# The decayed factors of the queries: from a transfer of their own to two ScalarE exponentials a chunk

## The chip, the core and the metric

The kernel runs on one core of a Trainium2 chip. A core has five engines that each run their own instructions in order and wait for one another by semaphores: PE (TensorE, matmuls; its weight loads are listed as PEld), DVE (VectorE), ACT (ScalarE), POOL (GpSimd) and SP (SyncE, which here issues most transfers). Transfers are carried out by 16 DMA engines. The metric is the device time of one execution in microseconds (us), the median of the runs.

## The reference

One transformer block over `x` of shape 8 x 2048 x 256. The part that the change touches is the attention, a linear attention with a decay for each head (16 heads of 64 columns) and each token:

```python
h = layernorm(x) * (1 + ca) + sa
q = elu(h @ Wq) + 1 ; k = elu(h @ Wk) + 1 ; v = h @ Wv
a = sigmoid(h @ Wa + ba + 2)          # one decay for each head and token
for t in range(2048):                  # for each batch and head
    S = a[t] * S + outer(k[t], v[t]) ; z = a[t] * z + k[t]
    out[t] = (q[t] @ S) / (q[t] @ z + 1e-6)
x = x + ga * (out @ Wo)
```

After it come a second layer norm and a mixture of 8 experts (256 x 256 each), of which every token uses two, and a second gated addition.

## The kernel before, in words

The 2048 tokens of a batch are cut into groups of 256 tokens (`GT`), and a group into two chunks of 128 tokens (`C`). There are 64 groups. The recurrence is done by chunks: inside a chunk the scores of keys and queries are multiplied by the decay between the two tokens and by the values; what comes from earlier chunks is the state `S` multiplied by the queries, each query having been multiplied by the decay since the chunk's start.

Both decays come from one row for each head, `le`, the running sum of the negative logarithms of the decays in the chunk. `decays` (L343 to L381) makes it on a tile of 64 rows (two chunks of 32 rows), and before the change also its exponential `exp(-le)` as a second plane of the same tile (L371). Both planes go to a DRAM tensor `led` (L374). `chunk_decays` (L400 to L418) is a generator that a chunk advances in steps:

1. it issues the transfer of `le` for all 16 heads to all 128 partitions, into `dec` (128 x 2048, 1 MB, L405);
2. it issues two transfers of `exp(-le)`, each of eight heads to one half of the partitions, into `el` (128 x 1024, twice 256 KB, through `spread_pairs`, L395): partitions 0 to 63 hold the first head of each pair, 64 to 127 the second;
3. POOL replaces the entries of `dec` above the diagonal in place by a large number (`affine_select`, L409);
4. in four steps of four heads, ACT makes `dec = exp(-dec + lt)` in place (L415), the decay between two tokens.

`el` is then read by POOL: its last column becomes the chunk's `whole` decay (L1056), and `el` is multiplied by the queries in place (L1048). PE reads it in `from_state` (L548). `dec` is multiplied by the scores on DVE (L501) and read by PE in `outputs` (L565).

The order of the instructions on every engine is the order in which the program is written (a manual schedule); nothing is moved by a scheduler. One pass of the main loop works on several groups at once: `here` (the scores, values and state of its chunks c0 and c1), `ahead` (the next group: its keys and queries), `coming` (the one after: its decays) and `prev` (the last one: its expert routing). Between them stand up to five places in a pass where an expert tile is loaded, turned and applied (`expert_tiles`), and `fetch_outputs`, which gathers expert results with indirect transfers from POOL. Two places of a pass matter here, both of them a single `advance` of `chunk_decays`:

- **`advance(own)`**, after c0's values and the layer norm rows of `prev`, and ahead of c0's `from_state` and `outputs`. It does step 3 for c1. ACT's neighbours there are `lnn_f` (L288) before, and after it eight of the exponentials of step 4 and then `lowk`, the first of four evictions of the key projection (L336, L337). ACT's next work is `hT_f` (L308).
- **`advance(dk)`**, after the last key projection of `ahead` and ahead of its query projection. It does step 3 for the next c0. ACT's neighbours there are the copy `z` (L1148) before, and `lowq`, the first of four evictions of the query projection, after.

The projections `pk` and `pq`, the value projection `pv`, the expert tiles' `pxt` and `py`, and the output projection `pw` take turns in four PSUM buffers of one pool (`mm`). A matmul into a buffer waits until the tile that was in it has been read. For a key or query projection that is done by DVE, after ACT's relu and exponential (`kT` and `qT`, L338).

## Time and profile before

| | |
|---|---|
| Median of 3 runs | 3899.13 us (3888.24 to 3919.3) |
| Profiled execution | 3885.85 us, span of the trace 3884.1 us, mean granted PE clock 0.969 |
| Busy: PE / DVE / ACT / POOL | 91% / 68% / 54% / 48% |
| Moved by DMA | 712.09 MB, mean 183 GB/s |
| `dec<-led` | 128 transfers of 1024 KB |
| `el<-led` | 256 transfers of 256 KB |
| Exponentials into `dec` (ACT, L415) | 2048, 389 ns each |
| `affine_select` of `dec` (POOL, L409) | 128, 2007 ns each |

Busy time is the time in which an engine had an instruction of its own in progress. Instructions on one engine overlap a little, so that eight exponentials of 389 ns take 2.44 us and not 3.11. A line of the timeline gives start, duration, engine, source line, operation, out<-in with the shapes, and how many alike were merged; in brackets stands the idle time of the engine before it and what ended that idle time. "issue" is idle time for which the profile shows no wait.

### The profile page before, as it was taken

The numbers are of one execution on the slowest core, as the hardware profiler recorded it, in microseconds if no ns is written. First come the engines' busy times: TensorE is split into PE (matmuls) and PEld (weight loads), VectorE is DVE, ScalarE is ACT, GpSimd is POOL, SyncE is SP. The second block draws the span as 40 slices with busy tenths as digits, with TensorE's granted clock in tenths as the row PEclk, the third lists the DMA queues.
The fourth block names the chain that finished last, engine by engine and source line by source line (L and its number), as shares of the span: only waits on it lengthen the run. The fifth ranks groups of instructions, "written<-read, shape, count | busy, mean of one in ns | idle before, by whom it ended". The sixth has DMA issues, their size and how long they took to land.

```text
span 3884.1 us, 82134 instructions
## 1 busy us (share of the span) xinstructions
PE 3546.7 (91%) x28998; PEld 2742.2 (71%) x28998; DVE 2640.0 (68%) x6396; ACT 2083.2 (54%) x5423; POOL 1846.2 (48%) x1986
## 2 busy tenths in 40 slices
PE   5999999999999999999999998999999999788786
PEld 3777777777777777777777776777777777666665
DVE  3777777777667667667766767767767767556555
ACT  3555555655555645655555655555655555444442
POOL 1444443443555454454545546445455444444554
PEclk9999999999999999999999999999999999989898
DMA  6444457666676666676576676576576576666766
GB/s 188 130 122 133 133 148 194 196 176 170 196 217 175 186 179 193 182 216 185 161 222 188 181 192 188 172 209 190 171 209 195 164 205 180 200 190 197 212 199 189
DMA packets 347404, 712.09 MB, mean 183 GB/s; under 512 B 43736, under 2 KB 212968, under 8 KB 322416
## 3 DMA queue, kind: packets, MB, share of 16 engines
q1 hardware_dynamic: 313488, 625.52, 57.5%
q0 software_dynamic: 27264, 74.49, 5.6%
q10 hardware_dynamic: 6240, 6.84, 0.6%
q8 instruction: 229, 3.75, 0.4%
q14 instruction: 183, 1.50, 0.1%
HBM read 577.29 MB, written 132.53 MB: 183 GB/s over the span
## 4 chain that ended last, share of the span: by engine, by line
PE 64%; DVE 15%; ACT 7%; issue 6%; DMA 3%; POOL 2%; SPq 0%; another core or an unknown queue 0%; DVEq 0%; ACTq 0%; POOLq 0%
PE pv L528 10%; PE pw L615 9%; PE pq L326 7%; PE pk L326 7%; PE po L565 6%; PE py L886 5%; PE sc L492 4%; PE ps L599 3%; PE po L548 3%; DVE at L433 3%; PE pd L449 2%; PE pk L511 2%; DMA xg<-xrows 2%; POOL at L1154 2%; ACT dec L415 2%
## 5 line engine op out<-in xcount | busy, mean ns | idle before, releaser
L415 ACT ACTIVATE dec<-dec,lt 128x128 f32<-128x128 f32 x2048 | 628.5, 389 | 14.2 <-POOL dec L409 14.2
L1154 POOL TENSOR_TENSOR at<-at,qT 128x512 f32<-128x512 f32 x256 | 326.1, 1285 | 579.2 <-DVE rmark L715 401.6
L326 PE MATMUL pk<-hT_a,wk_sb 128*128 128x256 f32 x2048 | 512.8, 395 | 5.0 <-issue 4.7
L326 PE MATMUL pq<-hT_a,wq_sb 128*128 128x256 f32 x2048 | 482.2, 389 | 13.2 <-DVE kT L338 12.5
L615 PE MATMUL pw<-wo_sb,oT 128*128 128x256 f32 x2048 | 478.0, 388 | 4.7 <-DVE oT L577 4.7
L528 PE MATMUL pv<-wv_sb,hT_a 128*128 128x512 f32 x1024 | 472.3, 604 | 2.5 <-DVE yg L890 2.3
L326 PEld LDWEIGHTS pq<-hT_a,wq_sb 128*128 128x128 f32 x2048 | 392.0, 194 | 75.4 <-DVE kT L338 19.4
L875 ACT ACTIVATE xgT<-pxt,modT,modT 128x128 f32<-128x128 f32 x622 | 245.0, 447 | 358.4 <-PE pxt L870 336.6
L615 PEld LDWEIGHTS pw<-wo_sb,oT 128*128 128x128 f32 x2048 | 393.5, 195 | 59.2 <-DVE oT L577 5.5
L326 PEld LDWEIGHTS pk<-hT_a,wk_sb 128*128 128x128 f32 x2048 | 381.1, 196 | 70.3 <-issue 13.3
L886 PE MATMUL py<-we,xgT 128*128 128x256 f32 x1244 | 348.4, 405 | 62.1 <-ACT xgT L875 28.3
L409 POOL TENSOR_SCALAR_AFFINE_SELECT dec<-dec 128x2048 f32<-128x2048 f32 x128 | 256.9, 2007 | 266.4 <-DMA dec<-led 201.8
L577 DVE TENSOR_TENSOR oT<-po,rb 128x512 f32<-128x512 f32 x256 | 173.1, 690 | 296.2 <-PE po L565 119.2
L433 DVE TENSOR_TENSOR_SCAN at<-at,z,kT 128x256 f32<-128x256 f32 x448 | 353.7, 830 | 2.0
L501 DVE TENSOR_TENSOR dec<-sc,dec 128x512 f32<-128x512 f32 x512 | 327.3, 682 | 36.8 <-PE sc L492 35.2
L528 PEld LDWEIGHTS pv<-wv_sb,hT_a 128*128 128x128 f32 x1024 | 189.8, 192 | 216.7 <-issue 174.2
L620 POOL TENSOR_TENSOR xt<-xt,dx 128x256 f32<-128x256 f32 x128 | 94.3, 737 | 480.2 <-DVE dx L619 479.9
L565 PE MATMUL po<-dec,v 128*64 128x128 f32 x4096 | 272.3, 278 | 36.1 <-issue 26.0
L886 PEld LDWEIGHTS py<-we,xgT 128*128 128x128 f32 x1244 | 227.5, 200 | 103.6 <-ACT xgT L875 35.7
L492 PE MATMUL sc<-qT,kT 64*128 64x128 f32 x4096 | 298.1, 286 | 0.1
L492 PEld LDWEIGHTS sc<-qT,kT 64*128 64x128 f32 x4096 | 250.1, 188 | 63.0 <-issue 62.8
L336 ACT ACTIVATE lowk<-pk 128x512 f32<-128x512 f32 x256 | 152.3, 595 | 257.0 <-PE pk L326 218.8
(199 smaller groups left out, 6208.2 us busy)
## 6 DMA issues: line engine op xcount, KB each, us to landing
dec<-led SPq DMA_DIRECT2D x128, 1024.0 KB
we<-ew_d SPq DMA_DIRECT2D x311, 384.0 KB
at<-ad SPq DMA_DIRECT2D x128, 512.0 KB
el<-led SPq DMA_DIRECT2D x256, 256.0 KB
rb<-rdd SPq DMA_DIRECT2D x128, 512.0 KB
xg<-xrows SPq DMA_DIRECT2D x311, 128.0 KB
yrows<-yg SPq DMA_DIRECT2D x311, 128.0 KB
xt<-in_L_attn_x_dram SPq DMA_DIRECT2D x64, 256.0 KB
```

The lines of the kernel that those rows point to most:

```text
L326: nc.tensor.matmul(pp[:, j * GT : (j + 1) * GT], w[:, k, (jj + j) * P : (jj + j + 1) * P], hT[:, k, :], start=(k == 0), stop=(k == KD - 1),)
L409: nc.gpsimd.affine_select(out=dec, in_=dec, compare_op=ALU.is_ge, fill=1e30, base=0, pattern=[[0, H], [1, C]], channel_multiplier=-1,)
L415: nc.scalar.activation(dec[:, h, :], dec[:, h, :], AF.Exp, scale=-1.0, bias=x.lt[:, 0, ch, h : h + 1])
L433: nc.vector.tensor_tensor_scan(zz[:, j, :], at[:, j, :], kT[:, j, :], 0.0 if z is None else z[:, j : j + 1], ALU.mult, ALU.add,)
L492: nc.tensor.matmul(sc[q][:, i, :], self.kT[rows, half * 4 + i, self.tok], self.qT[rows, half * 4 + i, self.tok], start=True, stop=True,)
L501: nc.vector.tensor_mul(w4, sc[q], w4)
L528: nc.tensor.matmul(pv, self.hT[:, k, self.tok], wv_sb[:, k, i * 512 : (i + 1) * 512], start=(k == 0), stop=(k == KD - 1),)
L565: nc.tensor.matmul(po[half * DH : (half + 1) * DH, i, :], self.v[:, h * DH : (h + 1) * DH], self.dec[:, q * NP + j, :], start=(self.S is N ...
L615: nc.tensor.matmul(pw[:, :D], self.oT[:, j, :], wo_sb[:, j, :], start=(j == 0), stop=(j == NP - 1))
L875: nc.scalar.activation(self.xT[:, k, :], pt[:, k * P : (k + 1) * P], AF.Identity, bias=modT[3][:, k, b : b + 1], scale=modT[4][:, k, b : b ...
L886: nc.tensor.matmul(py[:, :D], self.xT[:, k, :], self.w[:, k, :], start=(k == 0), stop=(k == KD - 1))
L1154: nc.gpsimd.tensor_mul(zz[:, part, :], zz[:, part, :], ahead.qT[:, part, :])
```

## The change

The exponentials `exp(-le)` are no longer made on the 64-row tile and no longer sent through DRAM. In their place ACT makes them from `dec`, which holds `le` on all partitions before POOL masks it: two instructions a chunk, each on 64 partitions and 8 heads x 128 tokens. `le` and `led` lose their second plane, the two transfers into `el` and the generator's step for them are gone, and the step of `affine_select` now begins with the two exponentials.

```diff
-        le = wk2.tile([R2, 2, C], F32, tag="le", name=f"le_{tag}", bufs=2)
-        nc.vector.tensor_tensor_scan(le[:, 0, :], ones[:R2, :C], e, 0.0, ALU.mult, ALU.add)
+        le = wk2.tile([R2, C], F32, tag="le", name=f"le_{tag}", bufs=2)
+        nc.vector.tensor_tensor_scan(le, ones[:R2, :C], e, 0.0, ALU.mult, ALU.add)
...
         yield
-        nc.scalar.activation(le[:, 1, :], le[:, 0, :], AF.Exp, scale=-1.0)
-
-        led = dram.tile([2, R2, C], F32, tag="led", name=f"led_{tag}", bufs=4)
-        nc.sync.dma_start(out=led.rearrange("n r t -> r n t"), in_=le)
+
+        led = dram.tile([R2, C], F32, tag="led", name=f"led_{tag}", bufs=4)
+        nc.sync.dma_start(out=led, in_=le)
...
-        nc.sync.dma_start(out=dec, in_=led[0, ch * 32 : ch * 32 + H, :].partition_broadcast(P))
+        nc.sync.dma_start(out=dec, in_=led[ch * 32 : ch * 32 + H, :].partition_broadcast(P))
         yield dec, el
-        spread_pairs(el, led[1, ch * 32 : ch * 32 + H, :])
-        yield
+
+        for q in range(2):
+            part = slice(q * DH, (q + 1) * DH)
+            nc.scalar.activation(
+                el[part], dec[part, q * NP : (q + 1) * NP, :], AF.Exp, scale=-1.0
+            )
         nc.gpsimd.affine_select(
             out=dec, in_=dec, compare_op=ALU.is_ge, fill=1e30, base=0,
             pattern=[[0, H], [1, C]], channel_multiplier=-1,
...
                 dk = chunk_decays(ahead.led, ahead, 0)
                 ahead.dec_el[0] = next(dk)
-                next(dk)
...
                 ahead.rb = next(dn)
-                next(ahead.dk)
```

More of the change, by code (lines that the diff above doesn't have):

```diff
@@ L362, in decays @@
         nc.vector.tensor_sub(e, e, y)
-        le = wk2.tile([R2, 2, C], F32, tag="le", name=f"le_{tag}", bufs=2)
-        nc.vector.tensor_tensor_scan(le[:, 0, :], ones[:R2, :C], e, 0.0, ALU.mult, ALU.add)
+        le = wk2.tile([R2, C], F32, tag="le", name=f"le_{tag}", bufs=2)
+        nc.vector.tensor_tensor_scan(le, ones[:R2, :C], e, 0.0, ALU.mult, ALU.add)
         left = wk2.tile([R2, C], F32, tag="left", name=f"left_{tag}", bufs=1)
         nc.vector.tensor_tensor(
-            left, le[:, 0, :], le[:, 0, C - 1 : C].to_broadcast([R2, C]), ALU.subtract
+            left, le, le[:, C - 1 : C].to_broadcast([R2, C]), ALU.subtract
         )
         yield
-        nc.scalar.activation(le[:, 1, :], le[:, 0, :], AF.Exp, scale=-1.0)
-        led = dram.tile([2, R2, C], F32, tag="led", name=f"led_{tag}", bufs=4)
-        nc.sync.dma_start(out=led.rearrange("n r t -> r n t"), in_=le)
+        led = dram.tile([R2, C], F32, tag="led", name=f"led_{tag}", bufs=4)
+        nc.sync.dma_start(out=led, in_=le)
         nc.scalar.activation(left, left, AF.Exp)
@@ L385, in by_token @@
         pc = small_tile(f"pc_{tag}")
-        nc.tensor.transpose(pc[:, :R2], le[:, 0, :], ident[:R2, :R2])
+        nc.tensor.transpose(pc[:, :R2], le, ident[:R2, :R2])
         nc.tensor.transpose(pc[:, R2 : 2 * R2], left, ident[:R2, :R2])
```

## The prediction

> **What bounds the kernel.** I read the page first: its busy row, and the chain of work that ended last by engine.

> ```profile
> PE 3546.7 (91%) x28998; PEld 2742.2 (71%) x28998; DVE 2640.0 (68%) x6396; ACT 2083.2 (54%) x5423; POOL 1846.2 (48%) x1986
> ...
> PE 64%; DVE 15%; ACT 7%; issue 6%; DMA 3%; POOL 2%; SPq 0%; another core or an unknown queue 0%; DVEq 0%; ACTq 0%; POOLq 0%
> ```

> PE is the bound, so nothing counts until it reaches PE. ACT's 46% of idle time proves little: DVE and ACT have 22% of the chain, where PE waits for an eviction. So I went to the timeline of one pass at the two places where the exponentials go in. First the place of c1, in a pass near 760 us (ACT's lines, then PE's):

> ```profile
> 759.60 1.09 ACT L288 ACTIVATE lnn_f<-xt,lns_f,lny_f 128x256 f32<-128x256 f32 x2
> 760.59 2.44 ACT L415 ACTIVATE dec<-dec,lt 128x128 f32<-128x128 f32 x8
> 764.90 0.60 ACT L336 ACTIVATE lowk<-pk 128x512 f32<-128x512 f32 x1 [1.87 <-PE pk L326]
> 766.07 1.01 ACT L308 ACTIVATE hT_f<-pn_f,modT,modT 128x256 f32<-128x256 f32 x2
> ...
> 767.09 1.03 PE L886 MATMUL py<-we,xgT 128*128 128x256 f32 x4
> ```

> ACT has 1.87 us to spare ahead of `lowk`. Behind it there is almost nothing: the eviction of `pk` ends with DVE's `kT` at about 766.9, and `py`, which takes that buffer, starts at 767.09. Then the place of the next c0, near 2041 us (ACT, DVE, PE):

> ```profile
> 2041.05 0.20 ACT L1148 COPY z<-at 128x4 f32<-128x4 f32 x1 [0.95 <-DVE at L433]
> 2041.69 0.60 ACT L336 ACTIVATE lowq<-pq 128x512 f32<-128x512 f32 x1 [0.45 <-DVE kT L338]
> 2042.33 0.63 ACT L337 ACTIVATE lowq<-lowq 128x512 f32<-128x512 f32 x1
> ...
> 2043.75 0.66 DVE L338 SCALAR_TENSOR_TENSOR qT<-pq,lowq 128x512 f32<-128x512 f32 x1
> ...
> 2050.11 0.69 DVE L338 SCALAR_TENSOR_TENSOR qT<-pq,lowq 128x512 f32<-128x512 f32 x1 [0.45 <-ACT lowq L337]
> ...
> 2050.86 1.13 PE L886 MATMUL py<-we,xgT 128*128 128x256 f32 x4 [0.18 <-DVE qT L338]
> ```

> From the first `qT` DVE has no pause for 4.6 us, then it waits for ACT, and PE waits for DVE. Last, what the transfers cost PE. In a later pass PE halts where no wait is shown (PE, then busy time by stretches: length, PE, PEld, DVE, ACT, POOL, granted clock, DMA share, GB/s):

> ```profile
> 2021.04 0.34 PE L565 MATMUL po<-dec,v 128*64 128x128 f32 x2 [0.47 <-issue]
> 2022.49 0.34 PE L565 MATMUL po<-dec,v 128*64 128x128 f32 x2 [1.10 <-issue]
> ...
> 2016.00:2025.00 9.00, 6.83 (x104) 5.07 (x103) 2.96 (x7) 4.02 (x12) 4.89 (x7) 1.00 1.05 321
> 2036.00:2053.00 17.00, 16.58 (x116) 13.37 (x114) 15.45 (x35) 11.76 (x29) 6.67 (x7) 1.00 0.16 46
> ```

> The halts fall where the DMA engines are full, and nearly all of the longer ones have one of PE's 16 KB instruction transfers within a few us. I count 36 passes of 64 with such a halt, about 110 us together, 2 to 4 us each, nearly all after 1080 us, when the gathers of expert results have begun.

> **What is removed.** 256 transfers into `el`, 67 MB of 712 MB; their issue on SP (median 595 ns, 152 us of SP); the exponential on the 64 rows (0.29 us, beside the 1.2 us in which ACT waits for DVE ahead of `z`: 0). The plane in `led` is 2 MB: 0. POOL's waits for `el` (105.7 us, 24 times, at `whole`) go, but `whole` and the product with the queries are done some 20 us before PE reads them: 0.

> **What an exponential costs.** On ACT 128 elements take 293 ns and 512 take 630 (L371, L337), 0.88 ns an element, so 1024 take 630 + 512 x 0.88 = 1.08 us. Neighbours overlap by 0.1 us, so a pair delays what follows by 1.96 us. 128 pairs are 251 us of ACT.

> **The place of c0.** The pair stands between `z` and `lowq`. `dec` was issued 16 us earlier, and POOL masks it without waiting at 2035.00, so it has landed. ACT's pause of 0.45 us takes part of the pair: `lowq` starts 1.44 us late. DVE comes to the first `qT` 0.79 us after the exponential's end, of which 0.76 can be used: it is 0.68 us late. Behind that lie DVE's chain, the second `z`, the last two `lowq`, the last `qT`, and `py`, which waits already: PE loses 0.68 us. I read both slacks pass by pass: 0.45 and 0.79 (or 0.67) in some 45 passes; in the first ten, without expert tiles, 0.45 and 0.46, so 1.0 us, and there it is PE's key transpose (L511) that waits for `qT`. In the last six with gaps of 2.6 us and more it costs nothing. Sum: 45 x 0.68 + 10 x 1.0 = **41 us**. POOL's mask now waits for the pair: from 2035.0 to 2043.2. Behind it stands only `at` times `qT` (L1154), which goes from 2044.5 to about 2045.3; its next one waits for the second `qT` anyway: 0.

> **The place of c1.** Here the pair, the mask and the exponentials of step 4 become a chain with nothing between: ACT makes the pair (1.96 us), POOL masks (2.0 us, formerly beside ACT's other work), ACT waits for it, with about 0.1 us for two handovers. Also queued behind ACT's wait are `lowk`, `hT_f` and `xgT`. The eight exponentials come 4.16 us later. ACT's pause ahead of `lowk` covers 1.87 us, `py` another 0.2, and PE loses 2.1 us. In the first ten passes `gate` waits for `hT_f` with no slack: 2.3. Where the pause is 0.8 to 1.2 us it is about 2.9. Over the 18 passes to 1080 us the pauses sum to 26.1 us: 18 x 3.96 - 26.1 = 45, less 1 for a `dec` that landed late. Later passes without a halt, and the end: 15. Passes with a halt have pauses of 3.5 to 7 us, because PE is late itself; they cover the 4.16 us except in some ten, for 5 us more. Sum: **64 us**. POOL's gathers (four, 1.25 us each) queue behind the mask and start 5.7 us later; their readers come 35 us after: 0. The state's decay (L584) also slips; the sum that needs it is 30 us off: 0.

> **The clock.** PE's granted clock halves after some stalls. [...] Of the 36 halts about 11 are followed by that, at some 2.5 us each. I take the trace: 27 new stalls of 2 to 3 us, 0.3 x 2.5 us each, some **18 us**.

> **The relief.** Without `el` the DMA engines are full some 2.3 us less a chunk (512 KB at 226 GB/s), and the gathers leave the stretch of the halt. [...] By the row it could be up to 110 us. But when a halt shrinks under 2.1 us, ACT's lateness at c1 takes its place: a floor. From 2.9 us to 2.1 in 36 passes is 29 us, and the clock falls that go with it up to 27. I take the middle, **-25 us**; bounds 0 and -56. SP's shorter queue may bring expert rows earlier (51 us of PE's waits for `xg`, mostly at the end): 0, at best -10.

> **Sum.** 41 + 64 + 18 - 25 = +98 us. The profiled execution took 3885.85 us (span 3884.1 and 1.75 around it), and would take 3984. It is 13 us under the median of the three runs; on the median the forecast is 3899 + 98 = 3997 us, 2.5% slower. Its own range is 3950 to 4045.

> **Rivals.** *Heavier:* no relief, and nearly every new stall brings the clock down: 41 + 64 + 27 x 2.5 = 173 us, 4072. [...] Against: only one in three did it.

> *Absorbed:* ACT's idle time swallows both places, and relief pays the rest: within 1%, about 3915. For it: the idle 46%. Against: the slacks above, alike in nearly all passes.

> *Relief wins, faster:* the floor at c1 doesn't hold, because PE gets past `py` without `kT`. Then the 64 us and their 18 of clock go, and all 110 us of halts and 27 us of clock return: 41 - 137 = -96, 3803; half of it, near 3850, is likelier. It decides from the point at which the relief exceeds the 41 us of c0. Against it: `py` does wait for `kT` in five passes already (11.9 us).

> *That it doesn't do what it says* is hardly possible: the order of ACT's instructions shows one pair in front of each mask. If `dec` lands after ACT gets there, ACT stalls with it; at c1 that is the case in about five passes, which are in the sum.

> **Chances.** Forecast 0.70, heavier 0.18, absorbed 0.08, relief 0.04. A measurement of this kernel tells about 1% from no change. The range leaves out the two light cases and reaches to the heavier one: 3930 to 4070. Slower by over 1%: 0.88; within: 0.08; faster: 0.04.

> **What would show it.** L415 with a wait for POOL's mask of about 2 us in nearly every pass, where it had 14.2 us in all; PE waiting for `kT` at `py` and for `hT_f` at `gate` by some 2 us in passes before 1080 us; PE's wait for `qT` at `py` near 0.9 us instead of 0.18; a pass in the early part 3 us longer than 50; DMA 65 MB less; halts under "issue" shorter. I am wrong if `py` or `gate` come with no more wait than now (c1 is covered), if `qT` isn't later (c0 is covered), or if the passes after 1080 us get shorter by more than those before get longer.

## The result, and the profile after

The changed kernel takes 3997.53 us (median, 3995.79 to 4003.36); the kernel before, run beside it on the same chip, 3895.95 us. The ratio is 1.0275 (95% interval 1.0246 to 1.0304), slower by 102 us where 98 were forecast. The changed kernel's profiled execution took 3997.27 us (span 3995.6, mean granted clock 0.949), 111 us more than the profile of before. The two profiles are compared below. DMA moved 642.86 MB, 69 MB less.

First the page of the changed kernel: the busy row, the chain of work that ended last by engine, and three groups (busy time and mean ns of one, then the idle time ahead of them and what ended most of it).

```profile
PE 3611.6 (90%) x28998; PEld 2798.6 (70%) x28998; DVE 2566.4 (64%) x6396; ACT 2311.9 (58%) x5615; POOL 1867.2 (47%) x1986
...
PE 46%; ACT 13%; DVE 12%; DMA 11%; issue 10%; POOL 7%; SPq 0%; DVEq 0%; POOLq 0%; ACTq 0%
...
L412 POOL TENSOR_SCALAR_AFFINE_SELECT dec<-dec 128x2048 f32<-128x2048 f32 x128 | 267.6, 2091 | 1117.3 <-ACT el L409 954.9
L418 ACT ACTIVATE dec<-dec,lt 128x128 f32<-128x128 f32 x2048 | 629.3, 389 | 135.1 <-POOL dec L412 135.1
...
L889 PE MATMUL py<-we,xgT 128*128 128x256 f32 x1244 | 358.0, 413 | 152.1 <-DVE kT L338 80.7
```

PE has 65 us more of busy time for the same 28998 matmuls: its mean granted clock is 0.949 where it was 0.969. On the chain its share falls from 64% to 46%, while POOL's goes from 2% to 7%. The row of L418 (L415 before) is the announced one: ACT waits 135.1 us for POOL's mask, 64 times and 2.1 us at most, so 2.1 us in every pass. PE's waits say who pays (us in total, times, longest), first before, then after:

```profile
PE po L565 <- issue: 26.0, 49, 1.1
PE ps L599 <- issue: 24.2, 44, 1.2
...
PE py L886 <- DVE kT L338: 11.9, 5, 3.0
...
PE pgate L628 <- ACT hT_f L308: 7.1, 4, 2.9
```

```profile
PE py L889 <- DVE kT L338: 80.7, 40, 2.7
...
PE pgate L631 <- ACT hT_f L308: 36.6, 16, 2.6
...
PE py L889 <- issue: 17.0, 12, 2.8
```

The timeline of the changed kernel at c1's place, in the pass near 760 us (ACT and POOL, then PE):

```profile
758.58 1.09 ACT L288 ACTIVATE lnn_f<-xt,lns_f,lny_f 128x256 f32<-128x256 f32 x2
759.57 2.11 ACT L409 ACTIVATE el<-dec 64x1024 f32<-64x1024 f32 x2
761.76 2.00 POOL L412 TENSOR_SCALAR_AFFINE_SELECT dec<-dec 128x2048 f32<-128x2048 f32 x1 [10.23 <-ACT el L409]
763.79 2.45 ACT L418 ACTIVATE dec<-dec,lt 128x128 f32<-128x128 f32 x8 [2.11 <-POOL dec L412]
766.15 0.57 ACT L336 ACTIVATE lowk<-pk 128x512 f32<-128x512 f32 x1
...
768.16 1.13 PE L889 MATMUL py<-we,xgT 128*128 128x256 f32 x4 [1.94 <-DVE kT L338]
```

Pair, mask and exponentials follow one another as the prediction drew them, and `py` stands still for 1.94 us. At the place of the next c0 it is otherwise:

```profile
780.29 0.20 ACT L1151 COPY z<-at 128x4 f32<-128x4 f32 x1
780.39 2.12 ACT L409 ACTIVATE el<-dec 64x1024 f32<-64x1024 f32 x2
782.53 0.60 ACT L336 ACTIVATE lowq<-pq 128x512 f32<-128x512 f32 x1
...
783.83 0.69 DVE L338 SCALAR_TENSOR_TENSOR qT<-pq,lowq 128x512 f32<-128x512 f32 x1 [0.76 <-ACT lowq L337]
784.63 0.28 DVE L723 TENSOR_TENSOR rpicks<-rpicks,rmark 128x32 f32<-128x32 f32 x1
...
790.74 1.13 PE L889 MATMUL py<-we,xgT 128*128 128x256 f32 x4
```

The pair is there, DVE waits for `lowq` by 0.76 us, but at the end `py` no longer waits at all. In the whole trace its wait for `qT` is 3.7 us in 10 passes, where it was 6.5 us in 36.

To see where the 111 us arise, I cut PE's time in passes 2 to 63 into three stretches: A from the sums of the denominators (`pd`) to the next key projection (`pk`), B from there to the decays' matmul (`pa`), which holds c1's place, and C from `pa` to `pd`, with c0's place. The clock loss is half of the time at half clock (the clock's records of both traces have 1.0 and 0.5 alone).

| stretch | before | after | difference | of it clock |
|---|---|---|---|---|
| A | 1701.7 us | 1621.5 us | -80.2 us | |
| B (c1's place) | 668.7 us | 867.6 us | +198.9 us | +85.6 us |
| C (c0's place) | 1201.2 us | 1190.9 us | -10.3 us | |

These add up to 108.4 us; the rest is in the start and the end. A's gain comes from the halts. PE's idle time under "issue" in A was 49.9 us in 29 passes, and none is left. Those 29 passes, clock loss taken out, were together 82 us longer than the common 25.28 us of A, in part because PE's matmuls also follow one another more slowly between the halts: those of `dec` and `v` (L565) start 59 ns apart there (mean, without the halts) and 55 ns in passes without a halt, those of the state (L599) 34 and 28 ns. Over the whole trace "issue" fell from 71.4 to 21.5 us, and 17.0 of the 21.5 us now lie at `py`, 12 times, where 40 other waits are for `kT`.

### The profile page after: what moved, and what is told of

It is laid out like the page before. It is cut to its first block, busy times and chain, and to the rows that moved or that the text cites. A ratio compares the mean times of both kernels' runs of the same rounds, so it can differ in the third digit from the quotient of the medians.

```text
span 3995.6 us, 81854 instructions
## 1 busy us (share of the span) xinstructions
PE 3611.6 (90%) x28998; PEld 2798.6 (70%) x28998; DVE 2566.4 (64%) x6396; ACT 2311.9 (58%) x5615; POOL 1867.2 (47%) x1986
## 2 busy tenths in 40 slices
DMA packets 322826, 642.86 MB, mean 161 GB/s; under 512 B 39640, under 2 KB 204776, under 8 KB 297840
## 4 chain that ended last, share of the span: by engine, by line
PE 46%; ACT 13%; DVE 12%; DMA 11%; issue 10%; POOL 7%; SPq 0%; DVEq 0%; POOLq 0%; ACTq 0%
PE pw L618 9%; PE pq L326 7%; DMA dec<-led 7%; PE pv L531 6%; PE py L889 5%; ACT dec L418 5%; PE pk L326 4%; POOL dec L412 3%; PE po L568 3%; PE sc L495 2%; DVE at L436 2%; POOL at L1157 2%; PE pd L452 2%; ACT el L409 2%; DMA xg<-xrows 2%
## 5 line engine op out<-in xcount | busy, mean ns | idle before, releaser
L412 POOL TENSOR_SCALAR_AFFINE_SELECT dec<-dec 128x2048 f32<-128x2048 f32 x128 | 267.6, 2091 | 1117.3 <-ACT el L409 954.9
L418 ACT ACTIVATE dec<-dec,lt 128x128 f32<-128x128 f32 x2048 | 629.3, 389 | 135.1 <-POOL dec L412 135.1
L618 PE MATMUL pw<-wo_sb,oT 128*128 128x256 f32 x2048 | 549.7, 430 | 4.5 <-DVE oT L580 4.5
L618 PEld LDWEIGHTS pw<-wo_sb,oT 128*128 128x128 f32 x2048 | 447.3, 222 | 80.3 <-DVE oT L580 5.5
L326 PE MATMUL pk<-hT_a,wk_sb 128*128 128x256 f32 x2048 | 495.7, 387 | 0.0
L889 PE MATMUL py<-we,xgT 128*128 128x256 f32 x1244 | 358.0, 413 | 152.1 <-DVE kT L338 80.7
L326 PE MATMUL pq<-hT_a,wq_sb 128*128 128x256 f32 x2048 | 484.3, 391 | 3.1 <-DVE kT L338 3.1
L326 PEld LDWEIGHTS pq<-hT_a,wq_sb 128*128 128x128 f32 x2048 | 394.0, 195 | 62.8 <-DVE kT L338 4.5
L326 PEld LDWEIGHTS pk<-hT_a,wk_sb 128*128 128x128 f32 x2048 | 371.7, 191 | 57.9 <-DVE dx L622 6.3
L338 DVE SCALAR_TENSOR_TENSOR kT<-pk,lowk 128x512 f32<-128x512 f32 x256 | 169.8, 682 | 295.3 <-ACT lowk L337 282.6
L436 DVE TENSOR_TENSOR_SCAN at<-at,z,kT 128x256 f32<-128x256 f32 x448 | 322.9, 762 | 2.1
L1051 POOL TENSOR_TENSOR el<-el,qT 128x1024 f32<-128x1024 f32 x120 | 284.7, 2372 | 5.5
```

The costliest lines, as they stand in the source:

```text
L326: nc.tensor.matmul(pp[:, j * GT : (j + 1) * GT], w[:, k, (jj + j) * P : (jj + j + 1) * P], hT[:, k, :], start=(k == 0), stop=(k == KD - 1),)
L412: nc.gpsimd.affine_select(out=dec, in_=dec, compare_op=ALU.is_ge, fill=1e30, base=0, pattern=[[0, H], [1, C]], channel_multiplier=-1,)
L418: nc.scalar.activation(dec[:, h, :], dec[:, h, :], AF.Exp, scale=-1.0, bias=x.lt[:, 0, ch, h : h + 1])
L436: nc.vector.tensor_tensor_scan(zz[:, j, :], at[:, j, :], kT[:, j, :], 0.0 if z is None else z[:, j : j + 1], ALU.mult, ALU.add,)
L618: nc.tensor.matmul(pw[:, :D], self.oT[:, j, :], wo_sb[:, j, :], start=(j == 0), stop=(j == NP - 1))
L889: nc.tensor.matmul(py[:, :D], self.xT[:, k, :], self.w[:, k, :], start=(k == 0), stop=(k == KD - 1))
```

## Experiments

Four questions: which place costs the time, why c0's place is free, what made the halts go, and what brings the clock down. The kernel before was run beside every one of them. The first four shared a chip on which it took 3885.65 us.

### One place at a time

c0's exponentials alone; c1 keeps its transfers. The other kernel is the same with `ch == 1` and the other `next` removed.

```diff
-        spread_pairs(el, led[1, ch * 32 : ch * 32 + H, :])
-        yield
+        if ch == 0:
+            for q in range(2):
+                part = slice(q * DH, (q + 1) * DH)
+                nc.scalar.activation(
+                    el[part], dec[part, q * NP : (q + 1) * NP, :], AF.Exp, scale=-1.0
+                )
+        else:
+            spread_pairs(el, led[1, ch * 32 : ch * 32 + H, :])
+            yield
...
                 ahead.dec_el[0] = next(dk)
-                next(dk)
```

> Only the next c0 gets its decayed factors from ScalarE; c1 keeps its transfers. The prediction's account: 41 us from the late first eviction of the query projection, less a relief of at most half of 25 us, so about +30 us, 3926 us. The theory after the trace of the changed kernel: PE's stretch from the decays' matmuls to the denominators was 0.37 us a pass shorter there, because the mask on POOL no longer lies beside DVE's work on the decays; the transfers that go here are not those issued just ahead of the halts. So -20 us, 3875 us, between 3850 and 3900.

> Only c1 gets its decayed factors from ScalarE; the next c0 keeps its transfers. Theory: the chain of pair, mask and exponentials at c1 is the whole cost, some 2 us of stall a pass at py or the gate and as much again by the halved clock, with most of the relief of the halts. So +110 to +130 us, near 4015 us, slower than the full change. The prediction's account with 41 us at c0: +98 - 41 = +57 us, 3953 us.

c0 alone: 3877.36 us, ratio 0.9985 (0.997 to 1.0). c1 alone: 3986.31 us, ratio 1.0262 (1.0215 to 1.0308). c1's place is the whole price, and the prediction's 41 us for c0 are not there. In passes 20 to 57 stretch C is even shorter with c0's pair, 705.0 us after 715.5, of which 3.6 us are clock. The halts stay with c0 alone (59.3 us under "issue", 43.4 of them in A). With c1 alone they are gone from A; of the 37.3 us that are left, 23.9 lie at `py`.

### Why c0's place is free

The trace of before, near 775 us: POOL's mask, and DVE's subtraction in the decays of `coming` (L362), which runs beside it.

```profile
774.08 2.00 POOL L409 TENSOR_SCALAR_AFFINE_SELECT dec<-dec 128x2048 f32<-128x2048 f32 x1
775.35 0.87 DVE L362 TENSOR_TENSOR ae<-ae,ay 64x128 f32<-64x128 f32 x1 [1.55 <-ACT ae L361]
```

DVE's operation ends 0.14 us after the mask; 50 of the 64 in that trace start while the mask runs, and each of those ends 0.14 us after it (median length 1.30 us). All of them in before, with two that come later on DVE (durations in ns: least, median, most):

```profile
L362 DVE TENSOR_TENSOR ae<-ae,ay x64: 282/1171/1871, 46.1 to 3615.9; 64x128 f32<-64x128 f32 x64
...
L720 DVE TENSOR_TENSOR rpicks<-rpicks,rmark x62: 193/1289/2286, 156.8 to 3710.4; 128x32 f32<-128x32 f32 x62
...
L723 DVE CAST rrows<-places x62: 170/170/226, 158.4 to 3711.9; 128x4 int32<-128x4 f32 x62
```

and in the changed kernel:

```profile
L362 DVE TENSOR_TENSOR ae<-ae,ay x64: 282/284/852, 46.2 to 3724.9; 64x128 f32<-64x128 f32 x64
...
L723 DVE TENSOR_TENSOR rpicks<-rpicks,rmark x62: 191/276/1582, 162.9 to 3817.7; 128x32 f32<-128x32 f32 x62
...
L726 DVE CAST rrows<-places x62: 170/961/972, 164.4 to 3819.2; 128x4 int32<-128x4 f32 x62
```

The subtraction does the same work in 0.28 us where it took 1.17, `rpicks` in 0.28 where it took 1.29, and a cast takes 0.96 where it took 0.17. Together DVE gains 0.89 + 1.01 - 0.79 = 1.1 us a pass, more than the 0.68 us of lateness that the prediction charged it with. The balance, -0.4 us a pass, is what stretch C shows: 17.85 us where it took 18.22 (median of passes 11 to 19). The cause would be POOL: the pair makes the mask late, and the mask (782.58 to 784.87 us in that pass), with POOL's first product of `at` and `qT` behind it (to 786.10), now stands beside other DVE work: the cast runs from 785.17 to 786.13. To test it I took the kernel before and moved only the mask of c0 past `times_queries(0)`:

```diff
             expert_tiles(share[2])
-            advance(dk)
             advance(zk)
...
             times_queries(0)
+            advance(dk)
             advance(qp)
```

> The kernel before with c0's mask on POOL moved behind the first product of the denominators, 10 us later, nothing else. If POOL's mask slows DVE's subtraction for the decays, that takes 0.3 us instead of 1.31, and the chain from it over the running sums to the first query eviction is up to 1 us shorter a pass: PE's stretch from the decays' matmuls to the denominators 18.2 to 17.8 us, -20 to -30 us in all. If the slow subtraction has another cause it stays at 1.3 us and the time within 0.4%. Open: the mask may then slow what stands beside it at its new place, and the second product comes 2 us later.

3784.76 us, ratio 1.0081 (1.0065 to 1.0096) on another chip, where the kernel before took 3754.25. Its trace:

```profile
L362 DVE TENSOR_TENSOR ae<-ae,ay x64: 282/283/853, 46.2 to 3517.2; 64x128 f32<-64x128 f32 x64
...
L720 DVE TENSOR_TENSOR rpicks<-rpicks,rmark x62: 191/1285/1299, 158.1 to 3610.5; 128x32 f32<-128x32 f32 x62
...
L723 DVE CAST rrows<-places x62: 223/1678/3596, 159.7 to 3612.0; 128x4 int32<-128x4 f32 x62
```

The subtraction is fast again with nothing changed but the mask's place, so it was the mask beside it that lengthened it. But in the pass near 790 us the cast now lies beside the mask (794.20 to 795.88 us, the mask 793.86 to 795.86) and takes 1.68 us, and `rpicks` still takes 1.30 us (1.29 in the median) beside the product, which did not move (792.65 to 793.95, the product 792.62 to 793.90). DVE gains 0.9 us and loses 1.5, and stretch C grew by as much, from 18.2 to 18.9 us (median of passes 11 to 19). Here the mask's move helped and hurt by what it landed beside.

### What made the halts go

The prediction credited the transfers that were removed. Three kernels test it: before without `el`'s transfers and with nothing in their place (`el` is zero, so what the state adds to a chunk is left out of the result); the changed kernel with c1's pair and mask moved ahead of the norm of `prev`, out of the chain; and before with only the gathers of expert results moved later, behind c1's `whole`, its state product and decayed queries and one more step of the key projection.

```diff
-        el = wk2.tile([P, NP, C], F32, tag="el", name=f"el_{tag}", bufs=2)
+        el = els[ch]
...
-        spread_pairs(el, led[1, ch * 32 : ch * 32 + H, :])
```

> The kernel before without the transfers into el and without any work in their place (el is two tiles filled with zeros once, so the part from the state is left out of the result). It measures the relief by itself. If the transfers feed the halts, the 110 us of unexplained halts go and PE's stretch up to the key projection shortens by 2.9 us in the passes with gathers: -80 to -110 us with the clock, 3790 to 3815 us. If fetching instructions is hidden and the halts have another cause, 3896 us within 0.5%.

```diff
             expert_tiles(share[0])
+            advance(own)
...
                 prev.rows = next(nf)
-            advance(own)
```

> The full change, but the step of c1 (pair and mask) stands ahead of the layer norm of the previous group, so that ACT has the value copies and the norm rows between the pair and the eight exponentials. If the chain with nothing between is what costs, the stretch from the key projection to the decays is as before (9.9 us), the relief stays, and the time is 3896 - 80 - 10 = some 3806 us, at most 3850. If ACT's added 2 us a chunk cost wherever they stand, it stays within 1% of 3896 or above. Open risk: dec lands at about that time, and ACT waits for it ahead of the value copies.

```diff
-            if not late:
-                fetch_outputs()
             if here:
                 whole_decay(here, 1)
...
             advance(kp)
+            if not late:
+                fetch_outputs()
             fetch_x()
```

> The kernel before, its transfers into el kept, with one call moved: the gathers of expert results on POOL stand behind c1's whole decay, state product and decayed queries instead of ahead of them, so that they start some 6 us later or more. Theory now: the halts come from the gathers lying beside PE's short matmuls of outputs and state, and went in the changed kernel because the gathers queue behind the late mask. Then the 110 us of halts go here too and PE's stretch up to the key projection falls from 28.1 to 25.3 us: -80 us or somewhat more with the clock, 3790 to 3815 us. Rival: the halts belong to the load of the transfers before them, or come back in the key projection: within 15 us of 3886.

Without the transfers: 3866.16 us, ratio 0.9957 (0.9941 to 0.9973), 19 us. The halts stay, 67.1 us under "issue" where it was 71.4; two of PE's waits in that trace:

```profile
PE po L564 <- issue: 27.8, 59, 1.1
...
PE ps L598 <- issue: 23.5, 44, 1.2
```

So `el`'s transfers neither caused the halts nor, by leaving, end them. With the pair early: 3942.85 us, ratio 1.0153 (1.0106 to 1.0199). Stretch B is back at its 9.91 us a pass (median without the clock's loss; 12.03 in the changed kernel), so the chain at c1 is indeed what lengthens it. But the pair now comes before `dec` has landed. ACT's wait, and PE's behind it:

```profile
ACT el L409 <- DMA dec<-led: 137.6, 45, 7.5
```

```profile
PE po L568 <- ACT v L538: 55.0, 33, 7.5
```

One wait has taken the place of the other. The halts are back as well, 62.6 us with 40.6 in A, though `el`'s transfers are gone. What separates the kernels with halts in A (before, c0 alone, no transfers, pair early) from those without (c1 alone, the changed kernel) is c1's place. In the first four POOL's gathers start 3.4 to 6.9 us ahead of the key projection, beside PE's short matmuls of outputs and state; in the other two 2.1 us behind its start (medians of passes 22 to 57), and PE then stalls for 2 us at `py`. Of the 71.4 us of halts before, 55.4 come within 3 us of a gather's start.

The late gathers alone ran on the chip of the late mask: 3738.34 us, ratio 0.9956 (0.994 to 0.9973). But there the halts are missing already. "issue" is 0.6 us with the late gathers, and 0.6 us in the run with the late mask, whose gathers start 3.6 us ahead of the key projection. So gathers at that place don't make halts everywhere. What ends the halts where they occur, the gathers' new place or the stall itself, and what the halts are, stays open.

### What brings the clock down

In the changed kernel the pair was moved ahead of the step that makes `lnn_f`, so that this 1.09 us lies beside POOL's mask:

```diff
             advance(nf)
+            advance(own)
             if prev:
                 prev.rows = next(nf)
-            advance(own)
```

> The full change with the step of c1 moved ahead of the two norm rows on ACT (1.0 us): half of POOL's mask is covered, and the stall at py falls from 2.2 to some 1.2 us a pass. If the clock falls with every us of stall alike, the time falls by 64 x 1 us and half of the clock's loss, to some 3895 us. If it falls only by a stall that is long enough, nearly all of the clock's loss (about 85 us in that stretch) goes and the time is 3997 - 64 - 80 = some 3850 us. If the pair waits for dec there as it did ahead of the norm, it stays near 3940.

3843.34 us, ratio 1.0238 (1.0222 to 1.0254), on the chip of the late mask. The changed kernel had not run on a chip without halts, so its price there was not known. Both ran side by side on one more such chip, where the kernel before took 3754.75 us:

> The full change once more, beside the others on one chip. The kernel before takes some 3886 us on a chip where PE's halts occur and 3754 us on one where they do not (the last runs). On a chip without halts there is nothing to give back: the 64 stalls of 2.2 us and their clock come on top, 3754 + 3.8 x 62 = some 3980 to 3990 us, 6% slower, nearly the same time as with halts, because the late gathers remove the halts anyway. On a chip with halts 3997 us, 2.7% slower, as before.

> The full change with c1's pair ahead of the two norm rows, now beside the full change on one chip. If the clock falls only by a stall that is long enough, it is 64 x 1.0 us of stall and 70 to 85 us of clock below the full change, 140 us, 3850 us; if the clock's loss goes with the length of the stall, 64 + 40 us below. 3843 us on the chip without halts; here within 20 us of that whatever the chip, since the gathers are late here too.

The changed kernel takes 3970.82 us there, ratio 1.0567 (1.0543 to 1.0591); with the pair moved 3841.23 us, ratio 1.0229 (1.0203 to 1.0255). The cores' view and PE's wait for `kT`, first of the changed kernel on that chip:

```profile
die 0 (median of its cores): 3969.4 us, clock 0.954
...
PE py L889 <- DVE kT L338: 106.4, 50, 3.6
```

then of the one with the pair moved, with its place at 730 us:

```profile
die 0 (median of its cores): 3837.7 us, clock 0.977
...
PE py L889 <- DVE kT L338: 61.4, 50, 3.6
...
730.50 1.09 ACT L288 ACTIVATE lnn_f<-xt,lns_f,lny_f 128x256 f32<-128x256 f32 x2
...
732.59 2.44 ACT L418 ACTIVATE dec<-dec,lt 128x128 f32<-128x128 f32 x8 [0.99 <-POOL dec L412]
```

With the clock loss taken out, stretch B in passes 20 to 57 is 2.2 us a pass longer in the changed kernel than in the kernel with the late mask, which is as before there (531.0 - 376.6 - 70.0 over 38 passes), and 1.3 us with the pair moved (432.2 - 376.6 - 6.8). That one microsecond a pass is worth 130 us: some 58 of stall in B and 94 of clock, less 22 us by which C is longer with the pair moved; why C is, I did not find out. The clock loss in B over all passes is 111.0 us in the one and 17.0 in the other; between 60 and 3300 us the clock falls 49 times in the one and 18 times in the other. What such a fall looks like, in the trace of the changed kernel from the section on the result (`py`, then a stretch behind it: length, PE, PEld, DVE, ACT, POOL, granted clock, DMA share, GB/s):

```profile
1344.17 1.29 PE L889 MATMUL py<-we,xgT 128*128 128x256 f32 x4 [1.93 <-DVE kT L338]
...
1346.00:1352.00 6.00, 6.00 (x20) 5.17 (x21) 3.49 (x14) 3.38 (x12) 2.69 (x2) 0.51 0.38 115
```

PE is busy without a gap and gets through 20 matmuls in 6 us. The stall was over at 1344.17; the clock's record has the half clock from 1345.01 to 1351.83. In the trace of before the clock fell after a halt: the halt at 1205 to 1208 us is there in pieces (0.38, 0.46 and 1.12 us), and behind it PE got through 11 matmuls in 3.3 us at half clock, and through 21 in the next 3.3 us (PE, then the stretches as above):

```profile
1205.98 0.29 PE L599 MATMUL ps<-v,kd 128*64 128x64 f32 x2 [0.38 <-issue]
1206.73 0.29 PE L599 MATMUL ps<-v,kd 128*64 128x64 f32 x2 [0.46 <-issue]
1208.14 0.50 PE L599 MATMUL ps<-v,kd 128*64 128x64 f32 x9 [1.12 <-issue]
...
1209.30:1212.60 3.30, 3.30 (x11) 2.67 (x10) 0.24 (x1) 0.81 (x2) 2.90 (x2) 0.50 0.71 223
1212.70:1216.00 3.30, 3.30 (x21) 2.94 (x20) 2.35 (x4) 2.75 (x7) 0.35 (x1) 1.00 0.99 361
```

The clock's records of these two traces, before and the changed kernel from the section on the result, show which stalls it fell after. In each of them the falls behind the first 30 us, 42 and 71, start on one grid of 3.413 us (to within 0.01 us), and the half clock lasts one step of it 50 times and two steps 50 times, of 113. The stall above, 1.93 us, lies whole in the step from 1341.60 to 1345.01. The table counts steps at full clock between 60 and 3300 us by PE's idle time in the step; "fell" means that the clock fell at the step's end.

| PE idle in the step | kernel before: steps, fell | changed kernel: steps, fell | both: steps, fell |
|---|---|---|---|
| under 1.0 us | 840, 1 | 777, 0 | 1617, 1 |
| 1.0 to 1.5 us | 37, 3 | 30, 6 | 67, 9 |
| 1.5 to 1.95 us | 20, 8 | 44, 26 | 64, 34 |
| 1.95 us and over | 15, 15 | 18, 18 | 33, 33 |

So in these two traces the falls go with PE's idle time within one step: at 1.95 us and over the clock fell every time, under 1.0 us once in 1617 steps (PE's ends are modelled, so the edges are rough). A stall of 1.3 us alone stays under 1.5 us, where the clock fell in 10 steps of 1684; one of 2.2 us passes it, unless the grid cuts the stall in two, and there it fell in 67 of 97. Steps with 1.5 us and more number 35 in the kernel before and 62 in the changed kernel. That the clock fell 18 times with the pair moved, where the changed kernel has 49 falls, agrees with this.

### A version that beats both

c0's exponentials alone, and the gathers late:

> The exponentials for c0 alone (c1 keeps its transfers), with the gathers moved late as well. If the two add: the -6 us of c0 alone and the gain of the late gathers, about 5 us below the run with the gathers moved alone. The prediction's account of c0 (41 us of cost, no relief left to gain once the halts are gone): 40 us above it.

> The kernel before with the gathers of expert results moved late. Where the chip has the halts: they go, and with them the clock's falls, 3738 us as on the other chip, against 3886 us before (4% faster). Where it has none: 3738 against 3754 us as in the last runs. If the halts stay with moved gathers, 3870 us.

> The exponentials for c0 alone and the gathers moved late, once more. On a chip without the halts as in the last runs: 0.7% faster than before, 3729 against 3754 us. On a chip with the halts (before at 3886 us): if late gathers are what removes them, some 3735 us, 4% faster; if not, 3870 us, and the halts went in the full change because PE was standing still at py anyway.

Both edits: 3729.13 us, ratio 0.9926 (0.9912 to 0.9939), on the chip of the late mask; on yet another 3730.79 us, ratio 0.9941 (0.9927 to 0.9956), beside 3752.95. The gathers alone, on the chip of the last section: 3745.70 us, ratio 0.9974 (0.9964 to 0.9984). The version is 0.6 to 0.7% faster than the kernel before on chips where that one takes some 3755 us. It was not run on a chip with halts.

## Why the prediction was right, and where it was not

3997 us were forecast and 3997.53 measured. The direction and the chain at c1 were foreseen; that the sum is this close is luck, because two terms were far off, by 51 and 68 us, and cancelled.

- **c0's place, 41 us: wrong, -10 us.** The step that failed is "Behind that lie DVE's chain, the second `z`, the last two `lowq`, the last `qT`, and `py`, which waits already: PE loses 0.68 us". It carried DVE's durations over from before. They were 1.1 us a pass longer with POOL's mask and product where these stood before, and both moved with the pair; "from 2035.0 to 2043.2" was written down for the mask and priced on POOL alone. What the traces show is the durations: the subtraction takes 1.17 us (median) in before, beside the mask, and 0.28 in the two kernels whose mask stands elsewhere. With these durations the sum at c0 would have been 0.68 - 1.1, below nothing.
- **c1's place, 64 us, and relief, -25 us: right in sum, both larger.** In B the stalls are 198.9 - 85.6 = 113 us, in A -80: net 33 us against 39. The prediction had the passes with a halt cover c1's lateness, and the halts shrink to a "floor" of 2.1 us. The halts in A went entirely, so nearly every pass bears the stall. The reason given for the relief is refuted: without the transfers of `el` and any work in their place the kernel is 19 us faster, and the halts stay. No run shows the relief's bound of 0, from which its middle was taken; these 19 us are what was measured. The prediction's "about 110 us" of halts is more than the 71.4 us that PE's waits show under "issue".
- **Clock, 18 us: wrong, 86 us.** The step was "27 new stalls of 2 to 3 us, 0.3 x 2.5 us each". The stall comes in nearly every pass and not in 27, and the share of 0.3 was read from halts that come in pieces, while this stall is one piece: in B the clock falls 40 times after 10, from 60 to 3300 us. That a stall of 2 us costs clock at all held: in the traces of before and the changed kernel the clock fell after each of the 33 steps of 3.413 us in which PE was idle for 1.95 us or more.
- **Sum.** -10 + 33 + 86 = 109 us where 41 + 39 + 18 = 98 stood. Two of the forecast's own sums are off, and they nearly cancel too: 27 x 0.3 x 2.5 is 20 and not 18, and the middle of 0 and -56 is -28 and not -25.
- **Rivals.** *Heavier* named the right danger: where the kernel before takes 3754.75 us and there are no halts to lose, the change costs 216 us. *Absorbed* was right for c0, though not by ACT's idle time. *Relief wins* failed where it was said to: PE doesn't get past `py` without `kT`.
- **The signs.** All came but one: `py`'s wait for `qT` fell where 0.9 us was named, which is the sign that c0 is covered. The halts under "issue" did shrink, but not for the reason given. An early pass takes 54.2 us where 53 was named.

## What to carry to other kernels

An instruction put ahead of another engine's step makes a chain of what ran side by side; here pair (2.1 us), mask (2.0) and exponentials take ACT from 1.87 us of slack to 2.1 us of lateness, and moving one microsecond of other work into the wait returned 130 us. When a change moves a POOL instruction, read which DVE instructions lay beside it and which will, and take their undisturbed durations from the fastest of their kind in the same trace (here 0.28 us for a subtraction whose median was 1.17). Split a price into stall and clock, take the clock from what its records show (here falls after 33 of 33 steps of 3.413 us with 1.95 us of idle PE and more, after one of 1617 with under 1.0) and not from the mean of all stalls, and know whether the kernel before has halts: if they vanish with the change, they pay for part of it.
